# Gram products of an image's neighbourhoods in column groups of 32 tokens instead of 64, in a two-layer kernel on one Trainium2 core

## The chip, the cores and the metric

The kernel runs on one core of a Trainium2 chip. The metric is the device time of one execution in microseconds (us). A core has engines that run side by side, each in its own instruction order: TensorE (PE in the profile; its weight loads are listed apart as PEld), VectorE (DVE), ScalarE (ACT), GpSimd (POOL), and SyncE (SP), which here only issues DMAs. Engines wait for one another on semaphores.

## The reference, cut to what matters

Eight images `x` of 768 channels and 32x32 positions ("tokens", 1024 per image) pass through two residual layers, each on a group-normalised input. Layer 0 is an attention whose scores are made of the variances of keys and values:

```python
scores = var_v @ swapaxes(var_k, -2, -1) * scale      # 12 heads of 64, 1024 tokens
out = softmax(scores) @ v ; out = out @ W_proj.T + b_proj
```

Layer 1 is a 1x1 convolution over the feature and 28 local correlations of it:

```python
feat_n = feature / max(norm over channels, 1e-12)
corr = stack([sum(feat_pad[:, :, r:h+r, c:w+c] * feat_n, axis=1) for r, c in offsets()])
x = concatenate([feature, corr], axis=1) ; out = einsum('bchw,oc->bohw', x, conv_w) + conv_b
```

The 28 offsets are four lines of seven through a 7x7 neighbourhood: the two diagonals, the middle row and the middle column. A correlation is symmetric in its two tokens, so offsets that look ahead (up to three image rows down and three columns to either side) suffice.

## The kernel before, in words

Channels lie on 128 partitions by 6 (`[128, 6, 1024]`). The large products (keys, values, projection, convolution) are split in a Strassen-like way into seven products each; the line of all their matmuls is 350 and their PSUM tiles are called `x`, `y`, `z` and `own`. All matmuls are in f32, and every f32 matmul of the program is two PE instructions in the trace. Nearly all of them use 64 columns of the array at a time: two matmuls side by side, one for each half of the PSUM partitions.

**Order of work.** A planner at build time (`Clock`) keeps an estimated time for each engine and decides the order in which units are issued; `later.after(us, ...)` plans a piece of follow-up work for an estimated time. On the chip, the order of each engine is fixed and only semaphores hold anything back. Images overlap: while layer 0 of image b runs, layer 1 of image b-1 is worked in.

**Attention** (image b, six head pairs of two heads, eight token tiles ("steps") each). For each step ACT makes two exponentials `ex` (line 775, one for each head), and PE multiplies them with the values in four matmuls (`av`, line 801). The steps run on PE in runs of four, two runs for each pair. `expool` holds `ex` for three steps. For pairs 0 to 2 (pairs 1 and 2 in image 0) the softmax's denominators are made on ACT too, by a further exponential with an accumulator (`junk`, line 785, two for each step); for the others DVE adds the exponentials up (`acc`) and PE sums them over the partitions with 32-column matmuls (`den`, line 832). Step (1,3) below means head pair 1, step 3.

**Correlations of an image** (`Corr`, line 1126), for blocks t of 128 tokens, that is, four image rows:

- `turn` (1130) copies the block of all channels into two sides of 16 image columns each, `[128, 6, 2, 64]`. It is two POOL instructions (1143), for the last image two ACT copies (1140). `turnpool` has one buffer; the last image uses `expool`'s.
- `gram` (1145) multiplies each side's 64 tokens with a window of the image, 7 rows by 19 columns (133), in the last block 4 by 19 (76). That is 6 channel groups x 2 sides = 12 matmuls, 24 PE instructions (line 1159).
- `out` (1169) copies the product from PSUM to one of three `win` tiles (DVE; ACT for the last image) and sends it to DRAM in two DMAs of 64 partitions x 136 elements (1177). After four blocks `diagonals` (1185) reads the wanted diagonals back in four DMAs (`dd`), `scale` (1201) normalises them (POOL for `rn`, DVE for `dn`), and `to_dram` (1216) transposes them on PE (`ct`, line 353) and writes the rows out.
- `gather` (1234) reads the rows back in shifted order into `cs` and `v` by 14 DMAs, `product` multiplies them on DVE and copies the result to three more partition groups, and the convolution takes `cs` in further matmuls (1064, 1278).

For images 0 to 6 the eight grams are queued as `beside`, single units that the planner sets between units of the next image's keys, values and attention. For the last image there is nothing to set them beside: they run one after the other behind the first two convolution units (`rest += [first, start] + units[:2] + grams + units[2:17]`). There DVE makes `f_last` (the normalised feature) and then the summed operands of the convolution's Strassen products (`t1f`, `t2f`, `t`, `t4f`), all at line 167.

Of the kernel before, what the change touches and what calls it, by code (L numbers as in the profile page):

```python
# [6 lines left out]
F32 = mybir.dt.float32  # L7
AF = mybir.ActivationFunctionType
ALU = mybir.AluOpType
# [4 lines left out]
P = 128  # L14
NB, C, H, W = 8, 768, 32, 32
N = H * W
J = C // P
NH, HD = 12, 64
HP = NH // 2
MT = N // P  # L20
HF = N // 2
# [6 lines left out]
RUNS = ((0, 0, 4), (31, -1, 3), (62, -2, 5), (93, -3, 7))  # L28
HW = W // 2
TALL, WIDE = MT // 2 + 3, HW + 3  # L30
AHEAD_OF = [o for first, _, count in RUNS for o in range(first, first + count)][1:]
NA = len(AHEAD_OF)
PAD = 99
SPAN = TALL * WIDE
WIN = SPAN + 3
# [18 lines left out]
TAIL = 0.0  # L54
EXP, SUM, STEP_US = 1.07, 1.15, 1.73
KV_US, T_US, CORR_US = 1.93, 2.58, 1.2
GRAM_US, TURN_US = 1.4, 2.3
WARM, BRIDGE = 42, (3, 7)


# [26 lines left out]
def windows(ap, *dims):  # L87

    return bass.AP(tensor=ap.tensor, offset=ap.offset, ap=[list(d) for d in dims])
# [83 lines left out]
def two_layers(ctx, tc, x, wkv, wproj, bproj, wconv, wcorr, bconv, out):  # L173
    nc = tc.nc

    def pool(name, bufs, **kw):
        return ctx.enter_context(tc.tile_pool(name=name, bufs=bufs, **kw))
# [10 lines left out]
    bcpool = pool("bcpool", 4)  # L188
    bkpool = pool("bkpool", 2)
    expool = pool("expool", 2 * AHEAD)  # L190
    turnpool = pool("turnpool", 1)
    wk = pool("wk", 3)
    uvpool = pool("uvpool", 1)
    st = pool("st", 1)
    xbank = pool("xbank", 2, space=PSUM)
    ybank = pool("ybank", 2, space=PSUM)
# [253 lines left out]

    rows = [dconst.tile([NROW, ROW], F32, name=f"rows{i}") for i in range(2)]
    windowed = [dconst.tile([MT, P * (PITCH + 2)], F32, name=f"windowed{i}") for i in range(2)]
    wins = [const.tile([P, WIN], F32, name=f"win{i}") for i in range(3)]
    for win in wins:
        nc.gpsimd.memset(win, 0.0)
    across = const.tile([W, NA], F32, name="across")
# [669 lines left out]
    class Corr:  # L1126
# [3 lines left out]
        def turn(self, t):  # L1130

            last = self.b == NB - 1
            pl, tag = (expool, "ex") if last else (turnpool, "turn")
            flat = pl.tile([P, N if last else J * P], F32, tag=tag, name=f"turn{self.b}_{t}")[:, : J * P]
            self.turned[t] = flat.rearrange("p (j s m) -> p j s m", j=J, s=2)
            to = flat.rearrange("p (j s y x) -> p j s y x", j=J, s=2, x=HW)
            rows = self.f[:, :, t * P : (t + 1) * P].rearrange("p j (y s x) -> p j y s x", y=4, s=2)
            for side in range(2):
                if last:
                    act_copy(0.5, to[:, :, side], rows[:, :, :, side, :])  # L1140
                else:
                    half = rows[:, :, :, side, :]
                    nc.gpsimd.tensor_tensor(to[:, :, side], half, windows(ones, ones.ap[0], (0, J), (HW, 4), (1, HW)), ALU.mult)  # L1143

        def gram(self, t):

            b = self.b
            tall = min(TALL, H - 4 * t)
            n = tall * WIDE
            if t not in self.turned:  # L1150
                self.turn(t)
            clock.turned = clock.now + GRAM_US + TURN_US
            block = self.turned[t]
            ps = other([P, SPAN], f"gr{b}_{t}")
            for j in range(J):
                image = self.f[:, j, :].rearrange("p (y x) -> p y x", x=W)
                for side in range(2):
                    left = side * (HW - 3)
                    nc.tensor.matmul(  # L1159
                        ps[side * HD : (side + 1) * HD, :n].rearrange("p (y x) -> p y x", x=WIDE),  # L1160
                        lhsT=block[:, j, side, :],
                        rhs=image[:, 4 * t : 4 * t + tall, left : left + WIDE],
                        start=j == 0, stop=j == J - 1,
                    )
            for ahead in range(t + 1, min(t + (3 if b == NB - 1 else 2), MT)):
                if ahead not in self.turned:
                    self.turn(ahead)

            def out():
                win = wins[t % 2 if t < MT - 1 else 2]  # L1170
                if b < NB - 1:
                    vector.tensor_copy(win[:, :n], ps[:, :n])
                else:
                    act_copy(0.3, win[:, :n], ps[:, :n])
                for side in range(2):
                    to = windowed[b % 2][t : t + 1, side * (HD * PITCH + HD - 3) :]
                    nc.sync.dma_start(
                        out=windows(to, (HW * PITCH - 3, 4), (PITCH, HW), (1, WIN)), in_=win[side * HD : (side + 1) * HD, :]
                    )
                if t % 4 == 3:  # L1180
                    later.after(4.0, lambda: self.diagonals(t // 4))

            later.after(GRAM_US + 0.25, out)

        def diagonals(self, hf):

# [14 lines left out]
        def scale(self, hf, dd):  # L1201

            b = self.b
            m = st.tile([P, 4], F32, tag="m", name=f"m{b}_{hf}")
            vector.tensor_scalar(m, dd[:, :, 0], NORM_EPS2, None, ALU.max)
            rn = st.tile([P, 4], F32, tag="rn", name=f"rn{b}_{hf}")
            nc.gpsimd.tensor_tensor(rn, m, neghalf, ALU.pow)

            def columns():
                dn = st.tile([P, 4, NROW], F32, tag="dn", name=f"dn{b}_{hf}")  # L1210
                vector.tensor_copy(dn[:, :, 0], rn)
                for q in range(4):
                    vector.scalar_tensor_tensor(dn[:, q, 1:NROW], dd[:, q, :], rn[:, q : q + 1], mask, ALU.mult, ALU.mult)
                later.after_dve(0.7 if b else 5.0 if hf else 7.5, lambda: to_dram(dn))

            def to_dram(dn):
                pt = small(f"ct{b}_{hf}")
                columns, over = dn.rearrange("p q r -> p (q r)"), 4 * NROW - HD
                turned(pt[0:HD, 0:P], columns[:, 0:HD])
                turned(pt[HD:P, 0:P], columns[:, over:])  # L1220
                cr = work([P, P], f"cr{b}_{hf}")
                vector.tensor_copy(
                    cr.rearrange("k (y s x) -> k y s x", y=4, s=2),
                    pt[:, 0:P].rearrange("k (s y x) -> k y s x", s=2, y=4),
                )
                for q in range(4):
                    at, row = PAD + hf * HF + q * P, q * NROW + (HD - over) * (q == 3)
                    nc.sync.dma_start(out=rows[b % 2][:, at : at + P], in_=cr[row : row + NROW, :])
                if hf == 1:
                    later.after(3.0, self.gather)  # L1230

            later.after_dve(2.5, columns)

        def gather(self):

            b, r = self.b, rows[self.b % 2]
            u = cs.rearrange("p a n -> p (a n)")[0:NCH, 0:N]
            v = uvpool.tile([NCH, N], F32, tag="uv", name=f"v{b}")
            nc.sync.dma_start(out=v[NS:NCH, :], in_=windows(r[0:1, PAD:], (0, NS + 4), (1, N)))
            nc.sync.dma_start(out=u[2 * NS : NCH, :], in_=windows(r[1:2, PAD:], (0, 4), (1, N)))  # L1240
            for n, (first, apart) in enumerate(PICKED):
                k, row = 3 * n, 2 + AHEAD_OF.index(first)
                nc.sync.dma_start(out=u[k : k + 3, :], in_=windows(r[row : row + 1, PAD:], (apart * ROW, 3), (1, N)))
                nc.sync.dma_start(out=v[k : k + 3, :], in_=windows(r[0:1, PAD + first :], (apart, 3), (1, N)))
                nc.sync.dma_start(
                    out=u[NS + k : NS + k + 3, :],
                    in_=windows(r[row : row + 1, PAD - first :], (apart * (ROW - 1), 3), (1, N)),
                )

            def product():  # L1250
                vector.tensor_tensor(u, u, v, ALU.mult)
                vector.tensor_tensor(cs[0:NCH, 2, :], cs[0:NCH, 0, :], cs[0:NCH, 1, :], ALU.subtract)
                for n in range(1, 4):
                    nc.sync.dma_start(out=cs[n * FOUR : n * FOUR + NCH, :, :], in_=cs[0:NCH, :, :])
                later.after_dve(6.0, lambda: ready.add(("cs", b)))

            later.after(18.0 if b < NB - 1 else 12.0, product)
# [167 lines left out]

    def turn_first():
        start_corr(0)
        later.after(6.0, lambda: ready.add("turned"))

    def project(b, ots, held=None):  # L1430
        f = first_f[0] if b == 0 else layer1[b - 1][0]
# [110 lines left out]
    def start_corr(b):  # L1542
        corrs.append(Corr(b, layer1[b][0]))
        corrs[-1].turn(0)

    second, corrs = [], []
    later.after(26.0, lambda: sum_weights(1, 9.0, 1.5))
# [4 lines left out]
    for b in range(NB + 1):  # L1552
# [8 lines left out]
        if b:  # L1561
# [8 lines left out]
            if b < NB:  # L1570
# [3 lines left out]
                        later.after(1.5 * n, lambda n=n: nc.sync.dma_start(out=f[:, n, :], in_=xv[b, :, n, :]))  # L1574

                conv.then = low_residual
            grams = [(GRAM_US if t < MT - 1 else 0.9, has_f if b > 1 else has_f + ("turned",), lambda t=t: (corr or corrs[0]).gram(t)) for t in range(MT)]
            first, start = (0.0, has_f, conv.sums.first), (0.0, (), conv.start)
            if b < NB:
                beside = grams  # L1580
# [68 lines left out]
```

## Time and profile before

| | us |
|---|---|
| median of 3 runs | 2582.31 (2581.68 to 2583.05) |
| the profiled execution's own time | 2580.96 |
| its span in the profile | 2579.2 |
| PE busy | 2571.7 |
| DVE / ACT / POOL busy | 1586.1 / 1418.3 / 424.4 |
| `gr` matmuls (line 1159) of images 0 to 6, busy | 83.6 (133 columns) + 7.5 (76) |
| granted PE clock | 1.0 of full speed |

In a group's line the numbers after the bar are the busy time and the mean duration in ns of one instruction, then the engine's idle time before those instructions and what ended it. In a timeline each line merges successive instructions of one kind: start, length, engine, line, operation and how many; idle time ahead of it stands in brackets. Matmuls overlap, so a matmul's duration is longer than the distance between two starts, and it is the distance that counts for the time.

### The profile page before, as it was taken

The page shows a single profiled execution, that of the slowest core. Times are in us where ns is not written, and L with a number is a line of the kernel's source. Part 1 is how long each engine was busy: PE and PEld are TensorE (multiplying, and loading weights), DVE is VectorE, ACT ScalarE, POOL GpSimd, SP SyncE. Part 2 cuts the span into 40 slices and gives each one's busy share as a digit, 9 for nine tenths or more (in the row PEclk, how much of TensorE's full clock was granted, in tenths as well). Part 3 has the DMA queues.
Part 4 walks back from the last instruction along what each step waited for, and adds up shares of the span by engine and source line. Part 5 has one row for each costly group of instructions (what it writes and reads, how often), then busy time and mean ns, then how long its engine had stood idle before and what let it go on. Part 6 is the DMA issues. An engine that isn't in the chain of part 4 may idle for free.

```text
span 2579.2 us, 40704 instructions
## 1 busy us (share of the span) xinstructions
PE 2571.7 (100%) x14798; PEld 1328.9 (52%) x14798; DVE 1586.1 (61%) x4101; ACT 1418.3 (55%) x1972; POOL 424.4 (16%) x449
## 2 busy tenths in 40 slices
PE   9999999999999999999999999999999999999999
PEld 5654356434764345643476434764347643575333
DVE  6868735775447853478534885358853577536864
ACT  1497279811697217971179711897118971189610
POOL 4320130004300043000430003300133001331000
PEclk9999999999999999999999999999999999999999
DMA  8766356355563655636556365563655636545333
GB/s 293 291 225 224 104 204 194 116 198 170 184 202 104 197 168 176 206 99 205 170 175 202 97 211 170 167 203 105 220 170 163 207 106 219 167 139 166 118 111 108
DMA packets 324718, 448.19 MB, mean 174 GB/s; under 512 B 59810, under 2 KB 245522, under 8 KB 324518
## 3 DMA queue, kind: packets, MB, share of 16 engines
q1 hardware_dynamic: 322454, 442.24, 53.1%
q10 hardware_dynamic: 2064, 3.34, 0.4%
q8 instruction: 118, 1.93, 0.3%
q14 instruction: 82, 0.67, 0.1%
HBM read 376.70 MB, written 64.40 MB: 171 GB/s over the span
## 4 chain that ended last, share of the span: by engine, by line
PE 97%; DMA 1%; ACT 1%; DVE 0%; SPq 0%; issue 0%; POOL 0%; ACTq 0%; POOLq 0%; DVEq 0%
PE x L350 34%; PE av L801 25%; PE y L350 17%; PE z L350 10%; PE own L350 5%; PE gr L1159 3%; PE den L832 1%; ACT ex L775 1%; PE warm L419 1%; DMA bc<-vdr 1%; ACT junk L785 0%; PE z L1064 0%; PE y L1064 0%; PE cc L1278 0%; DMA vdr<-rsv 0%
## 5 line engine op out<-in xcount | busy, mean ns | idle before, releaser
L775 ACT ACTIVATE ex<-bc,nk 128x1024 f32<-128x1024 f32 x768 | 826.9, 1137 | 398.8 <-DMA bc<-vdr 167.2
L801 PE MATMUL av<-ex,v 128*64 128x512 f32 x3072 | 694.2, 593 | 1.6 <-ACT ex L775 1.5
L801 PEld LDWEIGHTS av<-ex,v 128*64 128x64 f32 x3072 | 328.6, 137 | 322.7 <-issue 211.4
L785 ACT ACTIVATE junk<-bk,vm 128x1024 bf16<-128x1024 f32 x368 | 420.4, 1142 | 28.0 <-issue 10.7
L167 DVE TENSOR_TENSOR acc<-acc,ex 128x1024 f32<-128x1024 f32 x300 | 344.8, 1211 | 0.0
L350 PE MATMUL y<-kv,s 128*64 128x384 f32 x1488 | 265.3, 487 | 0.1
L350 PE MATMUL x<-kv,xn 128*64 128x384 f32 x1512 | 260.3, 486 | 0.0
L350 PE MATMUL x<-kv,s 128*64 128x384 f32 x1488 | 256.0, 486 | 0.0
L229 ACT COPY kp<-x 128x384 f32<-128x384 f32 x28 | 13.3, 478 | 404.7 <-PE x L350 395.9
L350 PEld LDWEIGHTS x<-kv,xn 128*64 128x64 f32 x1512 | 139.2, 137 | 104.6 <-issue 85.7
L350 PEld LDWEIGHTS x<-kv,s 128*64 128x64 f32 x1488 | 143.0, 137 | 92.7 <-issue 72.5
L350 PEld LDWEIGHTS y<-kv,s 128*64 128x64 f32 x1488 | 137.2, 137 | 88.6 <-issue 72.4
L530 POOL TENSOR_TENSOR rstda<-vea,neghalf 128x1 f32<-128x1 f32 x8 | 4.8, 595 | 950.8 <-DVE vea L167 950.8
L1143 POOL TENSOR_TENSOR turn<-f,ones 128x384 f32<-128x384 f32 x112 | 111.0, 1011 | 247.1 <-PE gr L1159 169.0
L350 PE MATMUL z<-kv,xn 128*64 128x384 f32 x768 | 134.2, 486 | 0.0
L350 PE MATMUL x<-f,wt 128*64 128x512 f32 x504 | 118.8, 592 | 0.0
L167 DVE TENSOR_TENSOR v<-y,v 128x128 f32<-128x128 f32 x180 | 40.9, 282 | 121.7 <-PE y L350 121.6
L636 POOL TENSOR_TENSOR s<-xn 128x384 f32<-128x384 f32 x64 | 65.0, 1026 | 293.3 <-PE x L350 181.7
L167 DVE BATCH_NORM_STATS2 vbn<-v 128x6 f32<-128x64 f32 x720 | 101.5, 209 | 0.0
L350 PEld LDWEIGHTS z<-kv,xn 128*64 128x64 f32 x768 | 75.0, 137 | 46.7 <-issue 36.1
L229 ACT COPY acc<-li 32x256 f32<-32x256 f32 x128 | 51.5, 402 | 82.9 <-DVE li L167 81.5
L1159 PEld LDWEIGHTS gr<-f,turn 128*64 128x64 f32 x1344 | 88.0, 136 | 11.9 <-issue 5.1
(205 smaller groups left out, 3132.5 us busy)
## 6 DMA issues: line engine op xcount, KB each, us to landing
kv<-kvs SPq DMA_DIRECT2D x124, 576.0 KB
kv<-in_wkv_dram SPq DMA_DIRECT2D x95, 576.0 KB
bc<-vdr SPq DMA_DIRECT2D x96, 512.0 KB
f<-in_x_dram SPq DMA_DIRECT2D x48, 512.0 KB
bk<-kdr SPq DMA_DIRECT2D x46, 512.0 KB
x1d<-f SPq DMA_DIRECT2D x42, 512.0 KB
xn<-x1d SPq DMA_DIRECT2D x42, 512.0 KB
out_dram<-xn SPq DMA_DIRECT2D x82, 256.0 KB
```

Source lines behind the costliest of these rows:

```text
L167: return getattr(self.engine, name)(*args, **kw)
L229: nc.scalar.copy(to, at)
L350: nc.tensor.matmul(out[at], lhsT=lhsT[:, at], rhs=rhs, start=start, stop=stop, **kw)
L419: nc.tensor.matmul(warm[:, 0:P], lhsT=ident, rhs=ident, start=True, stop=True)
L530: nc.gpsimd.tensor_tensor(self.rstd, ve, neghalf[:, 0:1], ALU.pow)
L636: nc.gpsimd.tensor_tensor(self.sums[g][:, 0], a[g][2], a[g][3], ALU.add)
L775: nc.scalar.activation(ex, self.bc[e], AF.Exp, scale=self.kv.nk[self.half][:, h, t : t + 1])
L785: nc.scalar.activation(junk, self.bk[e], AF.Exp, scale=self.kv.m2[self.half][:, h, t : t + 1], accum_out=self.sums[:, e, t : t + 1],)
L801: nc.tensor.matmul(self.av[hf][e * HD : (e + 1) * HD, :], lhsT=self.vt[:, t, e, :], rhs=exs[e][:, hf * HF : (hf + 1) * HF], start=t == 0, ...
L832: nc.tensor.matmul(den[at * 32 : (at + 1) * 32, :], lhsT=ones[:, 0:32], rhs=self.acc[e][:, hf * HF : (hf + 1) * HF], start=True, stop=True,)
L1143: nc.gpsimd.tensor_tensor(to[:, :, side], half, windows(ones, ones.ap[0], (0, J), (HW, 4), (1, HW)), ALU.mult)
L1159: nc.tensor.matmul(ps[side * HD : (side + 1) * HD, :n].rearrange("p (y x) -> p y x", x=WIDE), lhsT=block[:, j, side, :], rhs=image[:, 4 * ...
```

## The change

- A block's 128 tokens are multiplied in four groups of 32 (of each side, the upper and the lower two image rows) instead of two groups of 64. A group of two rows needs a window of 5 rows by 19 columns (95) instead of 7 by 19; the last block keeps 4 by 19. A gram becomes 24 matmuls on 32 columns each, 48 PE instructions.
- For images 0 to 6 two blocks' grams are issued in a row (`grams`), as four units instead of eight. `turnpool` gets two buffers, and blocks are turned two ahead.
- `win` has five tiles (four of 98 elements, one of 136). A block goes out in four DMAs of 32 partitions x 98 elements, the last block in two of 136.
- `uvpool` is gone: `v` in `gather` is two half tiles in `turnpool`, filled by ten DMAs instead of five, and `product` multiplies in two halves.
- The planned times change: those of a gram, a turn and the wait ahead of the columns' transposes `ct` (later by 4.3 and 2.8 in the planner's time for images 1 to 6, by 1.0 in the last one), and the first gram's condition in image 0 (6.0 becomes 8.0).
- In the last image the turned copy of side 0 stays on ACT and that of side 1 is made by DVE.

```diff
@@ constants and pools
-GRAM_US, TURN_US = 1.4, 2.3
+GRAM_US, TURN_US = (1.3, 2.4), 3.4
+SHORT = 2 + 3
-    turnpool = pool("turnpool", 1)
+    turnpool = pool("turnpool", 2)
-    uvpool = pool("uvpool", 1)
-    wins = [const.tile([P, WIN], F32, name=f"win{i}") for i in range(3)]
+    wins = [const.tile([P, WIN if i == 4 else SHORT * WIDE + 3], F32, name=f"win{i}") for i in range(5)]
@@ turn
             for side in range(2):
-                if last:
+                if last and side:
+                    vector.tensor_copy(to[:, :, side], rows[:, :, :, side, :])
+                elif last:
                     act_copy(0.5, to[:, :, side], rows[:, :, :, side, :])
@@ gram
+        def grams(self, t):
+            clock.turned = clock.now + GRAM_US[1] + TURN_US
+            for n in range(2):
+                self.gram(t + n)
...
+            groups = 4
+            tall = min(SHORT if groups == 4 else TALL, H - 4 * t)
...
-                for side in range(2):
-                    left = side * (HW - 3)
+                each = P // groups
+                for at in range(groups):
+                    side, low = divmod(at, groups // 2)
+                    left, first = side * (HW - 3), 4 * t + (0 if last else 2 * low)
                     nc.tensor.matmul(
-                        ps[side * HD : (side + 1) * HD, :n].rearrange("p (y x) -> p y x", x=WIDE),
-                        lhsT=block[:, j, side, :],
-                        rhs=image[:, 4 * t : 4 * t + tall, left : left + WIDE],
+                        ps[at * each : (at + 1) * each, :n].rearrange("p (y x) -> p y x", x=WIDE),
+                        lhsT=block[:, j, side, low * each : (low + 1) * each],
+                        rhs=image[:, first : first + tall, left : left + WIDE],
                         start=j == 0, stop=j == J - 1,
                     )
-            for ahead in range(t + 1, min(t + (3 if b == NB - 1 else 2), MT)):
+            for ahead in range(t + 1, min(t + 3, MT)):
@@ out
-                for side in range(2):
+                whole = last or groups == 2
+                size, count, down = (WIN, 4, 0) if whole else (SHORT * WIDE + 3, 2, 2 * (HW * PITCH - 3 + WIDE))
+                for first in range(0, P, count * HW):
...
@@ scale
-                later.after_dve(0.7 if b else 5.0 if hf else 7.5, lambda: to_dram(dn))
+                later.after_dve(1.7 if b == NB - 1 else (3.5 if hf else 5.0) if b else 5.0 if hf else 7.5, lambda: to_dram(dn))
@@ gather, product
-            v = uvpool.tile([NCH, N], F32, tag="uv", name=f"v{b}")
+            vs = [turnpool.tile([P, J * P], F32, tag="turn", name=f"v{b}_{hf}") for hf in range(2)]
...
-                vector.tensor_tensor(u, u, v, ALU.mult)
+                for hf, v in enumerate(vs):
+                    vector.tensor_tensor(cs[0:NCH, hf, :], cs[0:NCH, hf, :], v[0:NCH, :HF], ALU.mult)
@@ start_corr
     corrs[-1].turn(0)
+    corrs[-1].turn(1)
@@ the loop over images
-            grams = [(GRAM_US if t < MT - 1 else 0.9, has_f if b > 1 else has_f + ("turned",), lambda t=t: (corr or corrs[0]).gram(t)) for t in range(MT)]
+            if b < NB:
+                keys = has_f if b > 1 else has_f + ("turned",)
+                grams = [(GRAM_US[1], keys, lambda t=t: (corr or corrs[0]).grams(t)) for t in range(0, MT, 2)]
+            else:
+                grams = [(1.1 if t < MT - 1 else 0.9, has_f, lambda t=t: corr.gram(t)) for t in range(MT)]
```

More of the change, by code (lines that the diff above doesn't have):

```diff
@@ L1143, in turn @@
                     nc.gpsimd.tensor_tensor(to[:, :, side], half, windows(ones, ones.ap[0], (0, J), (HW, 4), (1, HW)), ALU.mult)
+        def grams(self, t):
+            clock.turned = clock.now + GRAM_US[1] + TURN_US
+            for n in range(2):
+                self.gram(t + n)
         def gram(self, t):
             b = self.b
-            tall = min(TALL, H - 4 * t)
+            last = t == MT - 1
+            groups = 4
+            tall = min(SHORT if groups == 4 else TALL, H - 4 * t)
             n = tall * WIDE
@@ L1151, in gram @@
                 self.turn(t)
-            clock.turned = clock.now + GRAM_US + TURN_US
             block = self.turned[t]
@@ L1169, in out @@
             def out():
-                win = wins[t % 2 if t < MT - 1 else 2]
+                win = wins[t % 4 if t < MT - 1 else 4]
                 if b < NB - 1:
@@ L1174, in out @@
                     act_copy(0.3, win[:, :n], ps[:, :n])
-                for side in range(2):
-                    to = windowed[b % 2][t : t + 1, side * (HD * PITCH + HD - 3) :]
+                whole = last or groups == 2
+                size, count, down = (WIN, 4, 0) if whole else (SHORT * WIDE + 3, 2, 2 * (HW * PITCH - 3 + WIDE))
+                for first in range(0, P, count * HW):
+                    side, low = divmod(first, HD)
+                    to = windowed[b % 2][t : t + 1, side * (HD * PITCH + HD - 3) + (down if low else 0) :]
                     nc.sync.dma_start(
-                        out=windows(to, (HW * PITCH - 3, 4), (PITCH, HW), (1, WIN)), in_=win[side * HD : (side + 1) * HD, :]
+                        out=windows(to, (HW * PITCH - 3, count), (PITCH, HW), (1, size)),
+                        in_=win[first : first + count * HW, :size],
                     )
@@ L1181, in out @@
                     later.after(4.0, lambda: self.diagonals(t // 4))
-            later.after(GRAM_US + 0.25, out)
+            later.after(GRAM_US[0 if b == NB - 1 else t % 2] + 0.1, out)
         def diagonals(self, hf):
@@ L1237, in gather @@
             u = cs.rearrange("p a n -> p (a n)")[0:NCH, 0:N]
-            v = uvpool.tile([NCH, N], F32, tag="uv", name=f"v{b}")
-            nc.sync.dma_start(out=v[NS:NCH, :], in_=windows(r[0:1, PAD:], (0, NS + 4), (1, N)))
+            vs = [turnpool.tile([P, J * P], F32, tag="turn", name=f"v{b}_{hf}") for hf in range(2)]
+            for hf, v in enumerate(vs):
+                nc.sync.dma_start(out=v[NS:NCH, :HF], in_=windows(r[0:1, PAD + hf * HF :], (0, NS + 4), (1, HF)))
             nc.sync.dma_start(out=u[2 * NS : NCH, :], in_=windows(r[1:2, PAD:], (0, 4), (1, N)))
@@ L1243, in gather @@
                 nc.sync.dma_start(out=u[k : k + 3, :], in_=windows(r[row : row + 1, PAD:], (apart * ROW, 3), (1, N)))
-                nc.sync.dma_start(out=v[k : k + 3, :], in_=windows(r[0:1, PAD + first :], (apart, 3), (1, N)))
+                for hf, v in enumerate(vs):
+                    nc.sync.dma_start(out=v[k : k + 3, :HF], in_=windows(r[0:1, PAD + first + hf * HF :], (apart, 3), (1, HF)))
                 nc.sync.dma_start(
@@ L1250, in product @@
             def product():
-                vector.tensor_tensor(u, u, v, ALU.mult)
+                for hf, v in enumerate(vs):
+                    vector.tensor_tensor(cs[0:NCH, hf, :], cs[0:NCH, hf, :], v[0:NCH, :HF], ALU.mult)
                 vector.tensor_tensor(cs[0:NCH, 2, :], cs[0:NCH, 0, :], cs[0:NCH, 1, :], ALU.subtract)
@@ L1427, in turn_first @@
         start_corr(0)
-        later.after(6.0, lambda: ready.add("turned"))
+        later.after(8.0, lambda: ready.add("turned"))
     def project(b, ots, held=None):
```

## The prediction

> **What bounds the kernel now.** First the page's busy row and its chain that ended last:
>
> ```profile
> PE 2571.7 (100%) x14798; PEld 1328.9 (52%) x14798; DVE 1586.1 (61%) x4101; ACT 1418.3 (55%) x1972; POOL 424.4 (16%) x449
> ...
> PE 97%; DMA 1%; ACT 1%; DVE 0%; SPq 0%; issue 0%; POOL 0%; ACTq 0%; POOLq 0%; DVEq 0%
> ```
>
> PE never rests, and the chain is PE's. A microsecond taken off PE counts, unless PE must then wait for something that now comes just in time. ACT has 55% over the whole span, which is an average. So next the windows by stage: image 3's first three head pairs, and the last image's end.
>
> ```profile
> 992.00:1084.00 92.00, 92.00 (x586) 56.56 (x583) 40.24 (x161) 89.95 (x121) 18.57 (x20) 1.00 0.56 174
> 2505.00:2579.00 74.00, 70.03 (x480) 29.20 (x476) 37.92 (x68) 8.83 (x24) 2.03 (x2) 0.99 0.38 110
> ```
>
> Columns: window, length, busy PE, PEld, DVE, ACT, POOL, clock, DMA share, GB/s. In the first window ACT is busy 89.95 of 92 us: there PE and ACT are level. ACT's timeline shows where they touch:
>
> ```profile
> 1005.24 1.15 ACT L785 ACTIVATE junk<-bk,vm 128x1024 bf16<-128x1024 f32 x1
> 1006.29 0.18 ACT L785 ACTIVATION_READ_ACCUMULATOR junk<-bk,vm 128x1 f32 x1
> 1007.44 2.19 ACT L775 ACTIVATE ex<-bc,nk 128x1024 f32<-128x1024 f32 x2 [0.96 <-PE av L801]
> ```
>
> These are step (0,7)'s two exponentials. They end at 1009.63; PE takes them at 1010.68. The cover is 1.05 us. Read the same way, it is 0.35 at (1,3), 0.88 at (1,7), 0.88 at (2,3), 0.55 at (2,7). Behind (2,7) ACT rests 0.56 to 3.9 us before the last step of each run.
>
> **PE's price of a gram.** Forms of line 1159 and of `den`, and two timelines:
>
> ```profile
> L1159 PE MATMUL gr<-f,turn 128*64 128x133 f32 x1176 | 83.6, 277 | 0.0
> L1159 PE MATMUL gr<-f,turn 128*64 128x76 f32 x168 | 7.5, 230 | 0.0
> L832 PE MATMUL den<-acc,ones 128*32 128x512 f32 x200 | 26.6, 605 | 0.0
> ```
> ```profile
> 997.00 1.55 PE L1159 MATMUL gr<-f,turn 128*64 128x133 f32 x24
> 998.36 4.06 PE L350 MATMUL x<-kv,xn 128*64 128x384 f32 x24
> ```
>
> A 133-column gram takes 1.36 us from its first start to the next unit's (998.36 − 997.00): 12 rounds of two matmuls side by side, 113 ns apart. The 76-column gram's rounds start 66 ns apart: 0.79 us. Between the two rows 95 columns cost 66 + 19 × 47/57 = 82 ns a round. The new gram has 48 instructions; if four run side by side that is again 12 rounds: **0.98 us**. That four can is seen in `den`, whose second four matmuls start 6.6 ns apart.
>
> `den` also shows a cost: from the last 64-column start before it (274.84) to the first behind it 1.52 us pass, where three rounds of 429 ns would take 1.29. Counted from the other of the two streams, the surplus is 0.35 to 0.40. So entering and leaving 32-column work costs 0.23 to 0.40; I take 0.32 for each pair of grams. A pair before is 2.72, after 2 × 0.98 + 0.32 = **2.28**; the pair of blocks 6 and 7 goes from 2.15 to 0.98 + 0.79 + 0.32 = 2.09. PE work per image falls by 3 × 0.44 + 0.06 = 1.38 us, 9.7 us for seven images.
>
> Bounds: no cheaper than two 76-column grams and the small surplus, 1.81. At worst matmuls come only as fast as the 76-column row shows them sustained, one per 33 ns: 48 × 33 = 1.58, a pair 3.5. I take 2.28, since the column count explains both `gr` rows and needs no issue limit. [...]
>
> **What becomes of it in an image** (image 3 worked out, 1 to 6 alike). Ahead of the first run of `av` stand, before, three grams and three `y` units; after, three pairs and two `y`: 3 × 2.28 − 3 × 1.36 − 1.93 = +0.83 (a unit of 12 matmuls is 1.93), so 990.13 becomes 990.96. ACT's work hangs on this run (its `ex` buffers) and has no gap up to 1006.48, so it is through at 1007.31; two `ex` of 2.19 end at 1009.50. PE now has, between the runs, the pair (6,7), two units and `ct` (0.22): 6.18 instead of 8.53. It stands at (0,7) at 1010.68 + 0.83 − 2.35 = 1009.16 and waits about 0.4. At (1,7): the fourth run starts 0.74 earlier than before (`gr7` is gone from ahead of it), PE is there at 1046.8; ACT's two `ex` end at 1047.25, since one `junk` (1.25) moved behind step (1,3) and nothing absorbs it. PE waits 0.5. At (2,7) ACT's rest of 0.32 absorbs a part; `ex` end at 1084.20, and PE starts there at 1084.30 instead of 1084.48. **Of 1.38 us an image keeps 0.19**; six keep 1.1. Each 0.1 that a pair costs more takes 0.3, as three pairs stand ahead of the first run.
>
> Image 0 has ACT just as full, but there a `junk` moves into an ACT rest of 2.9 us and another behind (1,7): 0.5 to 1.2 by the 1.38 and by the shift; I take 0.8.
>
> POOL's two copies of a turn (1011 ns each) come two blocks ahead, and POOL is busy 18.57 of 92 us: nothing, at most 0.25 at block 3, behind the transposed statistics. The window DMAs grow from 16 to 30 an image, `gather`'s from 14 to 19, all on SP, 0.3 to 0.5 us each: in images 0 to 6 `cs` is wanted more than ten us later, so nothing. `ct` moves 3 to 4 us back, so `dn` is there first. DVE's product in halves: nothing, for the same cover.
>
> **The last image.** Here DVE's queue decides:
>
> ```profile
> 2508.26 1.89 DVE L167 TENSOR_TENSOR t1f<-f_last 128x512 f32<-128x512 f32 x3
> 2510.06 1.28 DVE L167 TENSOR_TENSOR held<-z,held 128x512 f32<-128x512 f32 x2
> 2511.26 0.74 DVE L167 SCALAR_TENSOR_TENSOR f<-x,bconv_sb,f 128x512 f32<-128x512 f32 x1
> 2511.92 1.88 DVE L167 TENSOR_TENSOR t2f<-f_last,t1f 128x512 f32<-128x512 f32 x3
> ```
> ```profile
> 2510.96 7.08 PE L1159 MATMUL gr<-f_last,turn 128*64 128x133 f32 x120
> ...
> 2522.19 2.31 PE L350 MATMUL y<-t1f,wt 128*64 128x512 f32 x10
> ```
>
> DVE's half of the first turn is issued behind `held`, `f` and `t2f`, which end at 2513.7. An ACT copy of that shape took 0.505; so the half is there at about 2514.2, while PE wants it at 2510.96: **PE waits 3.2 us**. Then seven grams of 0.98, one of 0.79 and 0.3 for the switch: 7.95, with up to 0.6 for DVE's later halves: `y` at 2522.2 to 2522.8 instead of 2522.19. Eight grams took 11.23 before and 11.2 to 11.8 after: the 3.3 us saved pay the wait. Queued behind the halves are `t` and `t4f`: at most 8 × 0.5 = 4 us later, with over 15 us until PE wants them (`x<-t` at 2535.28). Behind `y` the correlations' chain (windows, `dd`, `dn`, `ct`, `gather`, `cs`) has 2.27 us of slack before `cc` (2561.35); `ct` later by 2.6 and five DMAs more use it up: 0.1 to 0.5. I take **+0.6** (−0.2 to +2.5). [...]
>
> **Sum.** −0.8 − 1.1 + 0.6 = −1.3 us on the profiled execution's 2580.96 (1.35 below the median): 2579.7; as a median **2581.0**. Every 0.1 us on a pair moves it by 2.5 (three pairs in each of seven images, and four in the last).
>
> **Rivals.**
> 1. *ACT gives way* (its wait at (0,7), (1,7), (2,7) is shorter because its queue does not hang on the first run): all of 9.7 − 0.6 stays: 2573.2. For it: ACT is 2.05 us below full in the window. Against: the 0.96 of rest lies ahead of (0,7) alone.
> 2. *32-column matmuls are held by issue*, each by its own load: place, the 28 pairs; price, 2.5 per 0.1 us; slower by over 0.2% from a pair of 2.54 on (−1.3 + 25 × 0.26 = +5.2). At 2.8 us 2594, at 3.5 us 2611. For it: one matmul per 33 ns is the fastest sustained row. Against: `den`.
> 3. *The change does less than it says*: a pair costs 2.4, the surplus larger: −1.3 + 3 = 2584, no change.
>
> **Chances.** Forecast (ACT eats most) 0.45, own range 2576 to 2586; rival 3 0.15; rival 1 0.20; rival 2 0.20. About 0.2% (5.2 us) is what a measurement of this kernel can tell from no change: faster below 2577.1, slower above 2587.5. Faster: rival 1 (0.20) and 0.05 of the forecast; slower: rival 2 but for the 0.01 that lies just short of 2.54; same the rest. Range: rival 1's value is kept, of rival 2 the lower half: 2573 to 2591.
>
> **What would show it.** After: `gr` with 128*32 and 128x95; a pair 2.28 long from start to next unit (above 2.5: rival 2); a new idle "PE av <- ACT ex" of about 1.2 us an image (none: rival 1); PE waiting 3.2 us for DVE's `turn` near 2511 and `y` within 1 us of 2522.2 plus the earlier images' shift. Wrong would be the walk if ACT's order or the planner's units in the run of `av` differ in other images from image 3's.

## The result, and the profile after

The changed kernel takes **2613.56 us** (median of 4, 2611.99 to 2621.02) against 2582.68 for the kernel before on the same chip: ratio 1.013, 95% interval 1.0118 to 1.0141. It is slower by some 31 us; 2581.0 and a range up to 2591 were forecast. The profiled execution took 2614.49, with a span of 2612.8.

From the page of after: the busy row, and the first of the chain's two rows. Then the three largest of PE's waits (engine and line, waited for, us in all, times, longest).

```profile
PE 2580.1 (99%) x16334; PEld 1187.0 (45%) x16334; DVE 1603.3 (61%) x4117; ACT 1413.0 (54%) x1964; POOL 423.2 (16%) x451
...
PE 89%; DVE 3%; DMA 3%; ACT 1%; SPq 1%; issue 1%; POOL 1%; DVEq 0%; ACTq 0%; POOLq 0%
```
```profile
PE ct L353 <- DVE dn L168: 16.2, 7, 3.0
PE gr L1170 <- DVE turn L168: 2.7, 1, 2.7
PE x L350 <- DVE kbn L168: 2.2, 6, 0.4
```

Before, PE's waits came to 3.5 us; now 16.2 stand at the transposes `ct`, which wait for `dn`. DVE's own waits for `dd` at `m`, the first step of `scale`, are 120.3 us in all, where they were 6.9. "PE av <- ACT ex", the wait that the prediction was built on, comes to 0.4 us. PE is also busy 8.4 us longer, though its grams are shorter. Where that is from shows in image 2 (the image whose grams run beside image 3's first head pairs), in four timelines. (`dd_0`, `m_0` and `ct_0` are those of an image's first half, blocks 0 to 3; `dd_1`, `m_1` and `ct_1` those of its second half.) First SP and DVE:

```profile
988.30 2.44 SPq L1191 DMA_DIRECT2D windowed<-win  x4
996.02 2.02 SPq L1206 DMA_DIRECT2D dd<-windowed  x4
998.09 8.76 SPq L1191 DMA_DIRECT2D windowed<-win  x14
1006.96 1.79 SPq L1243 DMA_DIRECT2D rows<-cr  x4
...
1009.99 2.42 SPq L1206 DMA_DIRECT2D dd<-windowed  x4
```
```profile
1015.25 0.17 DVE L168 TENSOR_SCALAR m<-dd 128x4 f32<-128x4 f32 x1 [10.65 <-DMA dd<-windowed]
1016.61 0.97 DVE L168 COPY dn<-rn 128x4 f32<-128x4 f32 x1 [1.19 <-POOL rn L1222]
1017.49 3.92 DVE L168 SCALAR_TENSOR_TENSOR dn<-dd,rn,mask 128x19 f32<-128x19 f32 x4
1021.33 0.87 DVE L168 BATCH_NORM_STATS2 kbn<-x 128x6 f32<-128x64 f32 x6
```

SP issues nothing from 990.7 to 996.02: the next in its queue is the first half's `dd`, which reads what the windows of blocks 0 to 3 are still writing. Behind it stand 14 window DMAs of blocks 4 to 7, 8.8 us of issue, though blocks 4 and 5 had been copied to `win` by 990.8. So the second half's `dd` goes out at 1009.99. DVE has reached `m`, which needs it, at 1004.6 and stands there for 10.65 us, with the statistics `kbn` of the next keys behind it.

Before, the same DMAs were spread out on SP, because the grams of blocks 4 to 7 stood on PE between 1004.2 and 1033. The second `dd` left 35 us behind the first, and not 14:

```profile
1003.02 2.03 SPq L1191 DMA_DIRECT2D dd<-windowed  x4
...
1038.24 2.02 SPq L1191 DMA_DIRECT2D dd<-windowed  x4
```

Now POOL and PE of the changed kernel:

```profile
1015.56 1.01 POOL L1222 TENSOR_TENSOR rn<-m,neghalf 128x4 f32<-128x4 f32 x1 [16.27 <-DVE m L168]
1016.54 1.97 POOL L636 TENSOR_TENSOR s<-xn 128x384 f32<-128x384 f32 x2
```
```profile
1016.49 2.14 PE L350 MATMUL x<-kv,xn 128*64 128x384 f32 x11
1021.46 0.44 PE L353 MATMUL ct<-ident,dn 128*64 128x128 f32 x4 [2.83 <-DVE dn L168]
1022.35 3.67 PE L350 MATMUL x<-kv,xn 128*64 128x384 f32 x12 [0.45 <-DVE kbn L168]
```

POOL's `s` (summed operands of the next keys' and values' products) were stuck behind `rn` and now run beside `dn`: DVE's four `dn` take 3.92 us here and 0.69 where POOL is still (at 999.70). PE waits 2.83 and 0.45 us, and then its 12 matmuls take 3.5 us to the next unit instead of 1.93. The windows of that stretch give the reason in the clock column (window, length, busy PE, PEld, DVE, ACT, POOL, clock, DMA share, GB/s):

```profile
1018.00:1021.40 3.40, 0.63 (x3) 0.00 (x0) 3.40 (x5) 3.37 (x6) 3.40 (x5) 1.00 0.95 361
1022.40:1024.00 1.60, 1.60 (x6) 0.78 (x8) 1.57 (x8) 1.60 (x2) 1.60 (x2) 0.50 0.32 130
1024.00:1026.00 2.00, 2.00 (x10) 0.85 (x8) 1.52 (x9) 1.69 (x4) 0.25 (x1) 0.64 0.02 5
```

Behind the wait the granted clock is halved; the record of the clock in the trace has 0.50 for 3.41 us from 1022.03 on. Set side by side, the starts of the `av` runs tell what the stall costs: run (0,4) of image 3 starts 2.03 us *earlier* than before, run (1,0) 4.70 *later*. Between these two runs images 3 to 7 take 5.7 to 6.7 us more than before, 31.6 in all (of each, 1.15 is other work: two units of 1.93 stand there in place of two grams of 1.36, and e10 has that too); image 2 takes 3.9 more, and image 1 takes less.

### The profile page after: what moved, and what is told of

Same layout as the page of the kernel before. It is cut to its first block, busy times and chain, and to the rows that moved or that the text cites. A ratio compares the mean times of both kernels' runs of the same rounds, so it can differ in the third digit from the quotient of the medians.

```text
span 2612.8 us, 43982 instructions
## 1 busy us (share of the span) xinstructions
PE 2580.1 (99%) x16334; PEld 1187.0 (45%) x16334; DVE 1603.3 (61%) x4117; ACT 1413.0 (54%) x1964; POOL 423.2 (16%) x451
## 4 chain that ended last, share of the span: by engine, by line
PE 89%; DVE 3%; DMA 3%; ACT 1%; SPq 1%; issue 1%; POOL 1%; DVEq 0%; ACTq 0%; POOLq 0%
PE x L350 32%; PE av L801 22%; PE y L350 17%; PE z L350 8%; PE own L350 5%; PE gr L1170 2%; DMA dd<-windowed 1%; ACT ex L775 1%; DVE dn L168 1%; PE den L832 1%; SPq L1191 1%; DMA windowed<-win 1%; POOL turn L1145 0%; DVE v L168 0%; DVE acc L168 0%
## 5 line engine op out<-in xcount | busy, mean ns | idle before, releaser
L801 PE MATMUL av<-ex,v 128*64 128x512 f32 x3072 | 706.9, 594 | 0.8 <-ACT ex L775 0.4
L801 PEld LDWEIGHTS av<-ex,v 128*64 128x64 f32 x3072 | 291.7, 137 | 373.5 <-issue 271.7
L350 PE MATMUL x<-kv,xn 128*64 128x384 f32 x1512 | 271.9, 497 | 2.2 <-DVE kbn L168 2.2
L350 PEld LDWEIGHTS x<-kv,xn 128*64 128x64 f32 x1512 | 126.5, 140 | 127.3 <-issue 101.8
L350 PEld LDWEIGHTS x<-kv,s 128*64 128x64 f32 x1488 | 133.9, 137 | 107.6 <-issue 91.4
L350 PEld LDWEIGHTS y<-kv,s 128*64 128x64 f32 x1488 | 122.7, 137 | 105.8 <-issue 86.4
L350 PE MATMUL x<-f,wt 128*64 128x512 f32 x504 | 124.7, 592 | 0.0
L168 DVE SCALAR_TENSOR_TENSOR xn<-x,bconv_sb,xn 128x512 f32<-128x512 f32 x63 | 46.4, 745 | 89.4 <-PE x L350 88.8
L350 PEld LDWEIGHTS z<-kv,xn 128*64 128x64 f32 x768 | 67.0, 137 | 57.6 <-issue 39.9
```

Of the source, the lines that this page charges most:

```text
L168: return getattr(self.engine, name)(*args, **kw)
L350: nc.tensor.matmul(out[at], lhsT=lhsT[:, at], rhs=rhs, start=start, stop=stop, **kw)
L801: nc.tensor.matmul(self.av[hf][e * HD : (e + 1) * HD, :], lhsT=self.vt[:, t, e, :], rhs=exs[e][:, hf * HF : (hf + 1) * HF], start=t == 0, ...
```

## The experiments

Eleven kernels ran, each against the kernel before on the same chip (median 2580.5 to 2580.6). Ratios have their 95% interval.

**e1: the transposes later.** PE's `ct` is moved out of the way of the late `dn`.

```diff
-later.after_dve(1.7 if b == NB - 1 else (3.5 if hf else 5.0) if b else 5.0 if hf else 7.5, lambda: to_dram(dn))
+later.after_dve(1.7 if b == NB - 1 else (12.0 if hf else 8.0) if b else 5.0 if hf else 7.5, lambda: to_dram(dn))
```

> The changed kernel with the columns' transposes planned later still (first half 5.0 becomes 8.0, second half 3.5 becomes 12.0 for images 1 to 6): on PE, ct_0 moves by 4 matmul steps and ct_1 behind the next run of av. Theory S (the 31 us come from PE standing at ct_1 for DVE's dn in images 2 to 6, 2 to 3 us each, and from the half clock that follows): no wait of PE for dn, granted clock 1.0 behind it, 5 x 5.6 = 28 us back: 2586 (2582 to 2590). Rival G (matmuls in groups of 32 columns, or the pairs' place in the order, cost the time themselves): 2608 or more.

Measured 2614.54 us, 1.0133 (1.0118 to 1.0148): nothing came back. `ct` has 8.5 to 10.2 us of cover now, but PE waits just as long a group of matmuls further on:

```profile
PE x L350 <- DVE kbn L168: 20.7, 6, 5.3
```

So theory S named the wrong wait. What PE stands for is whatever DVE has behind `m`: DVE's queue is the place, not `ct`. The time lies in rival G's range as well; G falls with e2 and e9, which keep both the groups and the pairs.

**e2: SP's queue.** The first half's `dd` are planned later, and on SP the windows of blocks 4 and 5 go ahead of them; nothing else is aimed at (PE's `ct_0` moves into the next `av` run, `ct_1` stays).

```diff
-                    later.after(4.0, lambda: self.diagonals(t // 4))
+                    later.after(4.0 if b == NB - 1 or t == MT - 1 else 9.0, lambda: self.diagonals(t // 4))
```

> The changed kernel with the first half's dd reads planned 5 us later, so that on SP the windows of blocks 4 and 5 go out ahead of them instead of behind; ct_1 stays where it is on PE. Theory S1 (what makes dn late is SP: the window DMAs stand behind dd_0, which waits for windows to land): dd_1 is issued about 4 us earlier (near 1006 instead of 1010 in image 2), PE's wait for dn at ct_1 falls under 1 us, clock stays 1.0: 2586 to 2592. Rival S2 (the landing of dd_1 behind 512 KB transfers, or DVE's dn beside POOL's s, 1.05 us each instead of 0.23, makes it late): ct_1 still waits over 1.5 us: 2600 to 2613.

Measured **2588.13 us**, 1.0029 (1.0018 to 1.0040): 7.5 us over its before instead of 31. SP and DVE of this kernel:

```profile
985.53 9.68 SPq L1191 DMA_DIRECT2D windowed<-win  x12
995.25 3.20 SPq L1206 DMA_DIRECT2D dd<-windowed  x4
998.55 3.71 SPq L1191 DMA_DIRECT2D windowed<-win  x6
...
1004.57 2.55 SPq L1206 DMA_DIRECT2D dd<-windowed  x4
```
```profile
1009.34 0.17 DVE L168 TENSOR_SCALAR m<-dd 128x4 f32<-128x4 f32 x1 [4.42 <-DMA dd<-windowed]
1010.70 0.96 DVE L168 COPY dn<-rn 128x4 f32<-128x4 f32 x1 [1.19 <-POOL rn L1222]
1011.58 3.94 DVE L168 SCALAR_TENSOR_TENSOR dn<-dd,rn,mask 128x19 f32<-128x19 f32 x4
```

The second `dd` is out at 1004.57 instead of 1009.99, `dn` is done at 1015.52, and `ct` starts at 1015.58: just in time. `dd` to `m` still takes 4.8 us and `dn` 3.94, so S2's two prices are real, but the 5.4 us on SP decide.

**e9: DVE's queue.** From e1, the second half's `m`, `rn` and `dn` are planned 8 us later; SP's order is that of the changed kernel.

```diff
-            later.after(6.0, lambda: self.scale(hf, dd))
+            later.after(14.0 if hf and 0 < b < NB - 1 else 6.0, lambda: self.scale(hf, dd))
```

> The kernel of e1 (transposes later) with the second half's scale (m, rn, dn) planned 8 us later too, so that on DVE m_1 stands behind the statistics kbn of the keys instead of ahead of them; SP's order with dd_0 ahead of the windows of blocks 4 and 5 stays. Theory Q (DVE stands at m_1 for dd_1, and what PE waits for is whatever DVE has behind m_1: dn in the changed kernel, kbn in e1): no wait of PE for kbn or dn over 0.5 us, clock 1.0: 2586 (2583 to 2591). Rival P (the order of the pairs or SP's late windows hold PE in another way): 2600 or more.

Measured **2585.14 us**, 1.0015 (1.0005 to 1.0024), 4.6 us over its before. SP is as late as ever (the second `dd` at 1008.42 in image 2), but the order of DVE has changed:

```profile
1013.75 0.86 DVE L168 BATCH_NORM_STATS2 kbn<-kp 128x6 f32<-128x64 f32 x6
1014.53 0.15 DVE L168 TENSOR_SCALAR m<-dd 128x4 f32<-128x4 f32 x1
...
1017.51 0.16 DVE L168 COPY dn<-rn 128x4 f32<-128x4 f32 x1
1017.57 0.68 DVE L168 SCALAR_TENSOR_TENSOR dn<-dd,rn,mask 128x19 f32<-128x19 f32 x4
```

`kbn` is ahead of `m`, `m` waits for nothing, and this `dn` takes 0.68 us. One long PE wait is left in these images, 2.4 us at a `ct_0` beside image 6. Two independent mends, one on SP and one on DVE, give back 23 and 26 us; so the chain "windows late on SP, DVE stands at `m`, PE starves behind DVE" is shown.

**e3: the groups undone, the order kept.** Two groups of 64, four wide `win` tiles, two window DMAs a block; PE's order is that of the changed kernel.

```diff
-            groups = 4
+            groups = 2
```

> The changed kernel with two groups of 64 tokens instead of four of 32: 133 columns, 12 matmuls a gram, two window DMAs a block (win is four wide tiles); PE's order is that of the changed kernel. Theory S: the order with ct_1 early is what costs; 8 window DMAs for blocks 4 to 7 instead of 14 bring dd_1 some 3.5 us forward, so the wait at ct_1 shrinks to 0 to 1.5 us, and a pair costs 2.72 instead of about 2.4: 2588 to 2600. Rival G (32-column groups cost the time themselves): 2580 to 2586.

Measured 2589.45 us, 1.0039 (1.0025 to 1.0052). With 8 window DMAs in place of 14 the second `dd` leaves SP at 1004.95 in image 2, and `ct` keeps 1.7 to 2.3 us of cover. So the order without the many small DMAs does not stall, and neither do the small DMAs without the order (e4, below); the changed kernel stalls because it has both.

**e4: the groups kept, the order undone.** Groups of 32 as eight single grams, `ct` 0.7 after `dn` as before.

```diff
-                grams = [(GRAM_US[1], keys, lambda t=t: (corr or corrs[0]).grams(t)) for t in range(0, MT, 2)]
+                grams = [(1.4 if t < MT - 1 else 0.9, keys, lambda t=t: (corr or corrs[0]).alone(t)) for t in range(MT)]
-later.after_dve(1.7 if b == NB - 1 else (3.5 if hf else 5.0) if b else 5.0 if hf else 7.5, lambda: to_dram(dn))
+later.after_dve(1.7 if b == NB - 1 else 0.7 if b else 5.0 if hf else 7.5, lambda: to_dram(dn))
```

> Four groups of 32 tokens in the order of the kernel before: single grams, planned at 1.4 us, and the transposes as early after dn as before (0.7); the rest as in the changed kernel (30 window DMAs, two turn buffers, last image with turned copies on two engines). Theory S: nothing waits; a gram of 0.92 us and a change of column groups each (0.3 to 0.5) against 1.36: 2579 to 2588. Rival G: 2600 or more.

Measured 2583.75 us, 1.0011 (1.0001 to 1.0021). From image 2 on, an image takes 0.37 us less than before (0.20 in one; not 0.18 each, as e6's expectation has it): a single gram of 0.9 us with the change of column groups at both its ends costs a little less than the 64-column gram did. At the end the profile is 3.0 us behind, so 4.2 are lost in the last image.

**e6, e7, e12: the last image.** e6 is e4 with the last image wholly as before; e7 is e4 with both turned copies on ACT; e12 is the kernel before with side 1 of those copies on DVE.

```diff
# e7 and (with 64-column groups, 2 window DMAs, ct 0.7 after dn in the last image) e6
-                if last and side:
-                    vector.tensor_copy(to[:, :, side], rows[:, :, :, side, :])
-                elif last:
+                if last:
# e12: the same lines put into the kernel before
```

> Groups of 32 as single grams in the order of before (e4), and the last image wholly as before: two groups of 64, two window DMAs a block, both turned copies on ACT, transposes 0.7 after dn. By the rows of e4, images 0 to 6 are 0.18 us each shorter than before, and the 4.2 us that e4 loses lie in the last image: 2579.5 against 2580.6 before (within 2 us). If the loss of e4 were in the images: 2583 or more.

> e4 with both turned copies of the last image on ACT again, its grams still in four groups of 32. Theory D (DVE's half stands in its queue: PE waits 2.7 us at the first gram): that wait goes; ACT's two copies and the window copy, 1.3 us a block, then pace the grams, 10.4 us for eight against 11.2 before; the wait of PE at ct_0 for dn (1.5 in e4, and the low clock behind it) moves with it or goes: 2579 to 2582. Rival W (30 window DMAs make dd and so dn late whatever the copies): the wait at ct_0 stays or grows, 2583 to 2585.

> The kernel before with one part of the change alone: in the last image the turned copy of side 1 is on DVE (grams in groups of 64, everything else as before). Theory D: PE waits 2.7 us at the first gram for DVE's half, which stands behind the summed operands in DVE's queue, and gets none of it back, as ACT's copies do not bound the grams much: 2583 to 2584 (before plus 2.5 to 3.2). Rival (the halves on two engines shorten the later grams' waits and pay it back): within 1 us of before.

Measured: e6 **2578.01** (0.9979 to 0.9998), e7 2581.53 (0.9993 to 1.0013), e12 **2584.56** (1.0006 to 1.0025). So in the last image DVE's half costs 2.2 us on top of 32-column groups (e4 less e7) and 4.0 by itself (e12 less its before; 2.8 by the rows of the profile), and the 32-column groups with their DMAs 3.5 (e7 less e6, which differ in the planned times of grams and `ct` too). PE of e12, then PE of e4, then SP of e7 (the grams of e7 and their waits take 9.9 us):

```profile
2510.36 0.39 PE L1161 MATMUL gr<-f_last,turn 128*64 128x133 f32 x2
2513.54 11.03 PE L1161 MATMUL gr<-f_last,turn 128*64 128x133 f32 x190 [2.79 <-DVE turn L167]
```
```profile
2512.90 9.63 PE L1175 MATMUL gr<-f_last,turn 128*32 128x95 f32 x367 [2.72 <-DVE turn L168]
...
2523.41 5.37 PE L350 MATMUL y<-t1f,wt 128*64 128x512 f32 x24
```
```profile
2510.63 17.00 SPq L1194 DMA_DIRECT2D windowed<-win  x27
...
2528.34 2.25 SPq L1209 DMA_DIRECT2D dd<-windowed  x4
```

Theory D's wait is there in e12 and e4, and gone in e7; nothing of it is won back. Rival W holds beside it: in e7 27 window DMAs take 17.0 us on SP, the first `dd` leaves at 2528.34 (2522.58 before), and PE waits 1.95 us at `ct_0`. The low clock that e7's expectation puts behind e4's `ct_0` is not there: the clock is 1.00 in 2538 to 2541, and it is behind e4's first wait that it falls (0.61 in 2513 to 2516).

**e8, e10: the parts put right.** e8 is e2 with the last image as before and one more mend: in the changed kernel and e2 the division of head pair 2's values (`v<-v,rd`, 1.22 us on DVE) had slid behind the convolution's residual sums, and DVE's `acc`, ACT's `ex` and PE's `av` came 1.1 us later in each of images 2 to 6.

```diff
-        self.rd_at = clock.now + {HP // 2: 8.0, HP - 2: 12.0}.get(self.hp, 14.0)
+        self.rd_at = clock.now + {HP // 2: 8.0, HP - 2: 12.0, 2: 12.0 if self.b > 1 else 14.0}.get(self.hp, 14.0)
```

> Pairs of grams in groups of 32 as in e2 (dd_0 behind the windows of blocks 4 and 5), the last image as before, and the division of head pair 2's values (v by rd on DVE) planned 2 us earlier, so that it stands ahead of the residual sums of the convolution again, as before. Theory: of e2's 7.5 us over before 4 to 5 lie in the last image and about 1 us in each of images 2 to 6 where ACT and PE wait for DVE's sums behind that division; both go and the pairs' gain of about 0.3 us a pair stays: 2574 to 2580. Rival (the pairs' order costs in images for another reason, three pairs ahead of the first av run or ACT): 2581 to 2586.

Measured **2574.22 us**, 0.9976 (0.9967 to 0.9986): faster than the kernel before. The 0.39 and 0.74 us that e2 loses at (4,4) and (5,0) of each image are 0.00 in e8. e10 adds e9's later `scale` (and `ct_1` 8.0 after `dn`):

> e8 (pairs in groups of 32, dd_0 behind the windows of blocks 4 and 5, division ahead of the sums, last image as before) with the second half's scale and transposes later as well, as in e9: DVE has the keys' statistics behind it before it stands at m_1. In e8 PE loses about 1.1 us in each of images 2 to 6, and 2.5 once, between the second run of av and the third: if that is DVE at m_1, 1 to 1.5 us an image go: 2567 to 2571. Rival (e8's residue is not m_1): 2573 to 2576.

Measured **2573.58 us**, 0.9971 (0.9959 to 0.9982), which cannot be told from e8. The rival holds. The 1.1 us of each image is work and not a wait: e10 has 1.15 in the same place with no wait there. And PE now waits at `ct_0` for `dn` beside images 4 to 6 (2.4 us in all).

**e11: the groups' own price.** e10 with two groups of 64 everywhere, the same order.

```diff
-            groups = 4 if b < NB - 1 else 2
+            groups = 2
```

> e10 with two groups of 64 in all images: the same order of all engines, only the grams of images 0 to 6 differ. This is the price of the groups alone, with nothing else waiting: by the traces a pair of 64-column grams is 2.72 and one of 32-column grams about 2.40 with its drain, so e10 plus 28 x 0.3 = 8 us: 2576 to 2579. Rival (ACT paces the attention and eats the gain, as the prediction had it): within 3 us of e10.

Measured 2579.20 us, 0.9996 (0.9987 to 1.0006), 5.6 us above e10 (7.3 by the profiled spans). That is 0.2 to 0.26 us for each of 28 pairs, waits included: e10 has its 2.4 us at `ct_0`, and the profile of e11 one wait of 2.4 us for POOL's `s` in image 0. In images 2 and 3, where neither kernel has such a wait, e10 gains 1.5 us an image, 0.38 a pair.

## Why the prediction was wrong

1. **The step that failed** is in the sentence on small costs: "The window DMAs grow from 16 to 30 an image … all on SP …: in images 0 to 6 `cs` is wanted more than ten us later, so nothing. `ct` moves 3 to 4 us back, so `dn` is there first." The end of the chain (`cs`) was held against its due time, and not each queue on the way. On SP the windows of blocks 4 to 7 stand behind a `dd` that waits for other windows to land; `m` on DVE stands in front of work that PE needs within microseconds. The order was misread too. In pairs, all eight grams of image 2 are through at 999.4, where the last one started at 1031.9 before; so on PE `ct_1` does not move 3 to 4 us back but 28 us ahead (1049.26 before, 1021.46 after), and its cover falls from 3.0 us to 0.05. Predicted 0; measured 23 to 26 us (e2, e9). In the profile of after the waits at `ct_1` and behind it are 2.5 to 3.5 us an image in five images, and the 12 matmuls behind them, at the halved clock, take 1.2 to 1.7 us more.
2. **The clock.** The forecast counted a wait of 3.2 us in the last image at its own length and had no lower clock in its sum. In the changed kernel PE waits 2.10 to 3.01 us beside each of images 3 to 7, with 0.19 to 0.45 us more behind it, and every time the clock is at 0.50 for 3.41 us from within 1.1 us of its end; the wait beside image 2, 1.56 and 0.45, left it at 1.00. In e9's last image it is halved behind a wait of 2.2 us. The clock's record is below.
3. **A pair of grams: right.** 2.28 was forecast. In e10 a pair takes 2.10 from its first start to the next unit's, with 0.10 more ahead of it and 0.06 behind: 2.26. The saving of 1.38 us of PE work an image was 1.5 in e10 against e11, in images without a wait. Rival 2, issue-bound matmuls at 1.58 us a gram, has the measured sign for a reason that does not hold: 96 instructions start in 2.10 us, one per 22 ns, where that rival has one per 33.

   In e10, PE's rows of one pair between two units:

```profile
980.45 4.04 PE L350 MATMUL x<-kv,s 128*64 128x384 f32 x24
984.42 2.17 PE L1168 MATMUL gr<-f,turn 128*32 128x95 f32 x96
986.51 7.09 PE L801 MATMUL av<-ex,v 128*64 128x512 f32 x32
```

   Here 24 matmuls take 3.97 instead of 3.87 before the column groups change, and 96 take 2.09.

4. **ACT eats the gain: wrong.** 1.2 us of waits an image were forecast; PE's idle time for `ex` is 0.4 us in the whole span of after and 0.6 in e10, and e11 shows the gain standing. ACT itself kept to the walk: at (0,7) of image 3 in after, its second `ex` ends at 1008.90, 18.47 us behind the start of the first run (18.54 in the walk), and PE stands there after 18.22 (18.20 in the walk). But the walk let PE wait for both exponentials of a step. A step begins with head 0, whose `ex` is there 1.1 us before head 1's, and each head has its own half of the columns: PE begins at 1008.65, and only head 1's matmuls start 0.31 later. Steps (1,7) and (2,7) start 1.87 us behind the step ahead of them instead of 1.72. So 0 to 0.16 us are left of the waits of 0.4 and 0.5. Rival 1 had the outcome, no wait, but not the reason: ACT's queue did hang on the first run.
5. **The last image: right on the wait, wrong on what pays it.** 3.2 us were forecast for DVE's half, 2.7 to 2.8 measured. "The 3.3 us saved pay the wait" failed: in e4 eight grams and their wait take 13.6 us (2509.82 to 2523.41) instead of 11.2, with the clock at 0.61 in 2513 to 2516 behind the wait, and `dn` comes 1.5 late for `ct_0`. The chain behind `y` was charged with `gather`'s five DMAs more, but not with the windows' 14: in e7 the first `dd` leaves 5.8 us later than before. Forecast +0.6; e4 against e6 says 5.7.
6. **An order that nobody aimed at.** That `v<-v,rd` slid behind the sums of the convolution was in DVE's order and was not looked at; it cost 5.7 us by the rows (five images of 1.13); no run has this mend alone.

What stays open: how much of the 3.3 us that `dn` loses beside POOL's `s` would by itself have spared the stall; that was not tried alone.

## What to carry to other kernels

When a change makes a transfer into more and smaller ones, do not ask only whether the last consumer has time: walk every in-order queue that the chain passes, ask what stands behind each waiting instruction there, and look at who needs that. Count what follows a wait, too: in after, waits of 2.1 to 3.0 us on TensorE beside images 3 to 7 came with 5.7 to 6.7 us more an image (1.15 of it other work), the clock at 0.50 for 3.41 us behind each. And where the order comes from a planner, compare the order of every engine and not only of the one that the change is about: two of the three mends here moved no work, they only put one instruction ahead of another.

## What the runs showed of the hardware that was not expected

- In after, DVE's small `scalar_tensor_tensor` (128x19) takes 0.23 us where POOL is still (999.70) and 1.03 to 1.05 beside POOL's `tensor_tensor` of 128x384 (1017.49), two of which take 1.97: four of DVE's take 0.68 in e9 and 3.92 in after. Even a 128x4 copy takes 0.97 there, and 0.16 in e9.
- Four 32-column groups work side by side: in after (988.52) their instructions start 6 to 7 ns apart, and the next four 82 ns behind the first. 48 instructions of 95 columns take 1.05 us (half of a pair's 2.10 in e10), against 1.36 for 24 of 133 in two groups before.
- How long PE waited did not by itself tell whether the clock fell. Behind a wait of 2.72 us in the last image it is halved in after and e4 (0.50, and 0.61 in 2513 to 2516) and 1.00 in e9; behind one of 2.79 us in e12 it is 1.00 up to 2519. Behind one of 3.38 us in e1, 12 matmuls take 1.96 us, not the 3.5 of after. In e9 a wait of 2.4 us near 1957 left it at 1.00 up to 1965, and one of 2.2 in the last image halved it. More shows in the clock's record of after: the halvings last 3.413 us and start at 1022.03, 1346.30, 1670.56, 1994.83 and 2319.09, each 95 times 3.413 us behind the last, and at 2544.37, 66 times on. Cut that trace into windows on this beat. From PE's first matmul to its last, six windows have PE idle for 2.43 to 3.01 us, and the clock is 0.50 behind each of them for one beat; in all others PE is idle for 1.79 us or less, and behind those it is 1.00. In e9 the last image's halving starts near 2537.8 (the clock is 0.55 in 2537.50 to 2540.00 and 0.80 in 2540.00 to 2543.00), seven beats behind 2513.87. Ahead of it PE is idle for 2.18 us in 2535.00 to 2537.50; the 1.99 us of the e9 window below left the clock at 1.00. So the wait of 2.72 us lies almost whole in one window in after, and the beat cuts it in two in e9 (PE's busy time is the second number behind the window, the clock the third from the end; after, then e9):

```profile
2540.96:2544.37 3.41, 0.88 (x44) 0.88 (x48) 3.41 (x8) 0.00 (x0) 0.00 (x0) 1.00 0.61 211
2544.37:2547.78 3.41, 3.41 (x98) 3.41 (x92) 2.70 (x6) 0.89 (x3) 0.00 (x0) 0.50 0.05 12
```
```profile
2510.45:2513.87 3.42, 1.43 (x71) 1.43 (x75) 3.42 (x9) 0.21 (x1) 0.00 (x0) 1.00 0.48 161
2513.87:2517.28 3.41, 3.41 (x173) 3.38 (x168) 2.69 (x6) 1.92 (x7) 0.00 (x0) 1.00 0.07 19
```

- On SP a window DMA takes 0.57 us of issue in after (median of 240, 224 of them of 32 partitions and 12.2 KB), no less than the 0.53 before (median of 128, of 64 partitions and 34.0 KB). By these medians the 30 of an image take 17.0 us of the queue where 16 took 8.4.
